# Gathering run 39's sums before its own scatter, and statistics one by one around output tiles, in a cross-attention and mixture-of-experts kernel

## The chip, the cores and the metric

The kernel runs on one core of a Trainium2 chip. The time is that of one execution on the device, in microseconds (us); of several executions the median counts. A profile is the record of one execution; its span goes from the first to the last instruction of the program. The engines are named as in the profile: PE is TensorE, PEld its weight loads, DVE is VectorE, ACT is ScalarE, POOL is GpSimd, SP is SyncE, which here only issues DMAs. The DMA queue q1 holds what SyncE issues, q0 what GpSimd issues; both are served by the same 16 DMA engines.

## The reference

The input x has 32 sequences of 128 tokens with 256 features, 4096 tokens in all. Layer 1 is a cross-attention on the normalised x, with 16 heads, added to x. Layer 2 normalises again, and sends each token through its best two of eight experts:

```
x = x + xattn(layernorm(x), ctx)                       # 16 heads of 64, then Wo, bo
r = layernorm(x)
logits = r @ Wg + bg
top2_vals, top2_idx = top_k(logits, 2)
combine = softmax(top2_vals) on the two experts
h = gelu(r @ W1[e] + b1[e])                            # 256 -> 1024, for each expert e
y = h @ W2[e] + b2[e]                                  # 1024 -> 256
out = sum over e of combine[e] * y[e]
result = x + layer_norm(r + out, gamma, beta)
```

All is in float32. So the last step of every token needs the outputs of both of its experts: the sum r + out, its mean and variance over 256 features, and then gamma, beta and the residual x.

## The kernel before, in words

The tokens are worked on in eight blocks of 512 for the attention and the choice of experts. Then each token is placed twice in a table in DRAM (`slots`), by expert. The feed-forward part takes that table in *runs*: a run is 256 tokens (two tiles of 128) or 128 tokens (one tile) of one expert. There are 46 runs, numbered in the order in which they are worked on. The last three (43 to 45) are spare and are skipped by a branch unless they are needed, so the last one that counts is number 42 (`L` in the code, `MAIN` is 43). `X` is 37. Runs 37 to 42 have two tiles each.

A run goes through four functions. `fetch_rows` has GpSimd gather the run's tokens by index. `turn` transposes them on TensorE and copies them out on VectorE (`xT`, L439). `hidden` multiplies by W1 and puts gelu on ScalarE (`hT`, L451 and L454). `outputs` multiplies by W2 (L470); VectorE adds the bias (L481), scales by the token's weight (L487), and GpSimd issues an indirect DMA which adds the tile's rows to a table of sums in DRAM, `total` (L490). This is called the scatter below. The scatters of two runs may not overlap, since a token may be in both: each run's scatter waits for the landing of the run before it. The two tiles of one run hold different tokens. `outputs` can be given a function (`then`) which is called once, behind its first tile.

The order on every engine is the order of the code: each engine works through a list written out by hand. PSUM has eight banks, which the tiles of all products use in turn.

The end of the kernel, where the change lies, runs two things side by side. On one hand, the blocks are finished: `load_sums` loads a block's 512 rows from `total` (L1105, SyncE), `measure` takes their statistics on VectorE (four pairs of L148 and L149, and a power of -0.5 on GpSimd, L155), `scale` normalises on ScalarE (L1128), and `put_out` multiplies by gamma and adds the residual on VectorE (L1134, L1141) and stores. For blocks 3 and 4 the residual is already in the output, so `put_out` stores with an accumulating DMA from GpSimd (L1145); for the others it is a plain store from SyncE (L1142).

On the other hand, blocks are loaded before all runs are added. Blocks 0 to 2 hold tokens of which runs up to 36 have all outputs; they are loaded behind run 36's scatter. Blocks 3 to 7 are loaded behind run 38's scatter. The tokens of the four runs 39 to 42 are then corrected one by one after the block's rows are written: for each of these runs `fetch_own` gathers the sums of its tokens from `total` (two indirect DMAs on GpSimd, L1166), `rate` takes their statistics (with a power on GpSimd, L1187), `patch` finishes them on VectorE (L1196, L1198), and `send` writes them over the output rows (two indirect DMAs on GpSimd, L1209, which wait for the writes of the run before). The residual rows are gathered earlier into `bases`. Runs 41 and 42 already spare a detour: run 41's outputs are kept in `kept_rows` and added on VectorE to sums gathered before its scatter (L1320), and run 42 is never scattered at all but added on VectorE (L484).

The order in the code around the change is: run 37's `hidden`, block 0's and 1's `measure`, run 37's `outputs` with block 2's `measure` inside; run 38's `hidden` and `outputs`; loads of blocks 3 to 7; run 39's `hidden` and `outputs` with measures of blocks 3 to 5; run 40's `hidden`, measures of blocks 6 and 7; the gather of run 39's sums; run 40's `outputs`; `rate` and `patch` of run 39; the gather of run 40's sums, `send` of run 39, the gather of run 41's sums; run 41's `hidden` and `outputs`; and so on to `send` of run 42.

Of the kernel before, what the change touches and what calls it, by code (L numbers as in the profile page):

```python
# [12 lines left out]
ALU = mybir.AluOpType  # L13
# [12 lines left out]
def kernel(  # L26
# [19 lines left out]
    nc = tc.nc  # L46
# [67 lines left out]
    total = dram.tile([NTOK + P, D], F32, name="total")  # L114
# [30 lines left out]
    def tile_stats(pool, src, mv, t):  # L145

        st = pool.tile([P, 6], F32, name="bnst", tag="bnst")
        nc.vector.bn_stats(st, src[:, t, :])  # L148
        nc.vector.bn_aggr(mv[:, t, :], st)  # L149

    def deviation(pool, mv, rstd):

        ve = pool.tile([P, TB], F32, name="ve", tag="ve")
        nc.vector.tensor_scalar_add(ve, mv[:, :, 1], LN_EPS)  # L154
        nc.gpsimd.tensor_tensor(rstd, ve, mhalf, ALU.pow)  # L155
# [18 lines left out]
    def bank(name):  # L174
        return ps.tile([P, TB, P], F32, name=name, tag="bank")

    def flat(t):
        return t.rearrange("p t s -> p (t s)")
# [5 lines left out]
    MAIN = NRUN - SPARE  # L184
# [223 lines left out]
    def reach(rows, m):  # L408

        return rows[: OLD * TOK, :] if m < AHEAD else rows  # L410
# [19 lines left out]
    def turn(m):  # L430

        nt, xg = order[m][2], rows_of.pop(m)
        px = flat(bank("px"))
        for k in range(KD):
            for t in range(nt):
                j = k * nt + t
                nc.tensor.transpose(px[:, ts(j, P)], xg[:, t, ts(k, P)], ident)  # L437
        xT = a2.tile([P, KD, nt * P], F32, name=f"xT{m}", tag="kT")
        nc.vector.tensor_copy(xT.rearrange("p k s -> p (k s)"), px[:, : KD * nt * P])  # L439
        turned[m] = xT  # L440
# [18 lines left out]
    added = []  # L459

    def outputs(m, then=None):


        nt, who, hT = order[m][2], whos.pop(m), hiddens.pop(m)
        mine = []
        w1t, bt, w2t = weights.pop(m)
        for t in range(nt):
            py = flat(bank("py"))
            for c in range(NHC):
                nc.tensor.matmul(  # L470
                    py[:, :D],
                    lhsT=hT[c // (NHC // 2)][:, c % (NHC // 2), ts(t, P)],
                    rhs=w2t[:, c, :],
                    start=(c == 0),
                    stop=(c == NHC - 1),
                )
            if m == MAIN - 2:
                y = kept_rows[:, t, :]
            else:
                y = f3.tile([P, D], F32, name=f"y{m}_{t}", tag="y")  # L480
            nc.vector.tensor_tensor(y, py[:, :D], bt[:, NHC:], ALU.add)  # L481
            if m == MAIN - 1:
                z = own(sums, m)[:, t, :]
                nc.vector.scalar_tensor_tensor(z, y, who[:, t, 1:2].bitcast(F32), z, ALU.mult, ALU.add)  # L484
                then(t)
                continue
            nc.vector.tensor_scalar(y, y, who[:, t, 1:2].bitcast(F32), None, ALU.mult)  # L487
            if t > 0:
                nc.gpsimd.memset(apart, 0.0)
            add = nc.gpsimd.indirect_dma_start(  # L490
                out=reach(total, m),
                out_offset=bass.IndirectOffsetOnAxis(ap=who[:, t, 0:1], axis=0),
                in_=y,
                in_offset=None,
                compute_op=ALU.add,
            )


            for other in mine:
                tc.declare_no_dep(add.ins, other.ins, reason="tokens of their own")  # L500
            for other in added:
                tc.add_manual_dep(add.ins, other.ins.name, DATA, reason="the run before")
            mine.append(add)
            if t == 0 and then is not None:
                then()
        added[:] = mine
# [540 lines left out]
    hidden(1)  # L1047
    turn(2)
    outputs(0, lambda: turn_gate(last))
    gate(last)  # L1050
    fetch_weights(3)
# [11 lines left out]
    route(last)  # L1063
    next(rest)
    outputs(1, lambda: next(rest))
    fetch_weights(4)
    next(rest)
# [32 lines left out]
    def load_sums(blk):  # L1100

        tag = ("qT", "xnT", "rows", "wkm", "wvm")[blk // 2 if blk < 6 else blk - 3]
        acc = (a2 if blk < 6 else aw).tile([P, TB, D], F32, name=f"acc{blk}", tag=tag)
        accs[blk] = acc
        got = nc.sync.dma_start(out=acc, in_=block(total, blk))  # L1105
        for other in added:
            tc.add_manual_dep(got.ins, other.ins.name, DATA, reason="these sums are complete")
        return got

    def measure(blk):  # L1110

        scales[blk] = (
            fs.tile([P, TB, 2], F32, name="mv3", tag="mv3"),
            fs.tile([P, TB], F32, name="rstd3", tag="rstd3"),
        )
        mv, rstd = scales[blk]
        for t in range(TB):
            tile_stats(fs, accs[blk], mv, t)
        deviation(fs, mv, rstd)
# [30 lines left out]
    L = MAIN - 1  # L1150
    X = MAIN - (NREST - EARLY + AHEAD)
    assert L - PATCH >= X + 1
    out_rows = out.rearrange("b s d -> (b s) d")
    sums = aw.tile([P, PATCH, 2, D], F32, name="sums", tag="wo_sb")
# [4 lines left out]
    def own(t, m):  # L1159
        return t[:, m - (L - PATCH + 1)]  # L1160

    def fetch_own(t, table, m, complete=()):

        who = last_who.setdefault(m, whos.get(m))
        for i in range(2):
            got = nc.gpsimd.indirect_dma_start(  # L1166
                out=own(t, m)[:, i, :],
                out_offset=None,
                in_=table,
                in_offset=bass.IndirectOffsetOnAxis(ap=who[:, i, 0:1], axis=0),  # L1170
            )
            for other in complete:
                tc.add_manual_dep(got.ins, other.ins.name, DATA, reason="these sums are complete")
# [3 lines left out]
    def rate(m, tiles=slice(0, 2)):  # L1177

        z = own(sums, m)[:, tiles, :]
        n = z.shape[1]  # L1180
        mv = fs.tile([P, 2, 2], F32, name="mvp", tag="mvp")
        ve = fs.tile([P, 2], F32, name="vep", tag="vep")
        rstd = fs.tile([P, 2], F32, name="rstdp", tag="rstdp")
        for t in range(n):
            tile_stats(fs, z, mv, t)
        nc.vector.tensor_scalar_add(ve[:, :n], mv[:, :n, 1], LN_EPS)
        nc.gpsimd.tensor_tensor(rstd[:, :n], ve[:, :n], mhalf[:, :n], ALU.pow)  # L1187
        parts[m, tiles.start] = mv, rstd

    def patch(m, tiles=slice(0, 2)):  # L1190

        z, base = own(sums, m)[:, tiles, :], own(bases, m)[:, tiles, :]
        mv, rstd = parts.pop((m, tiles.start))
        n = z.shape[1]
        for t in range(n):
            nc.vector.scalar_tensor_tensor(z[:, t, :], z[:, t, :], mv[:, t, 0:1], gamma_sb, ALU.subtract, ALU.mult)  # L1196
        for t in range(n):
            nc.vector.scalar_tensor_tensor(  # L1198
                z[:, t, :], z[:, t, :], rstd[:, t : t + 1], base[:, t, :], ALU.mult, ALU.add
            )  # L1200

    def send(m):

        z = own(sums, m)
        mine = []
        for t in range(2):
            if t > 0:
                nc.gpsimd.memset(apart, 0.0)
            put = nc.gpsimd.indirect_dma_start(  # L1209
                out=out_rows,  # L1210
                out_offset=bass.IndirectOffsetOnAxis(ap=last_who[m][:, t, 0:1], axis=0),
                in_=z[:, t, :],
                in_offset=None,
            )
            for other in mine:
                tc.declare_no_dep(put.ins, other.ins, reason="tokens of their own")
            for other in sent + [stored[blk] for blk in range(OLD, NBLK)]:
                tc.add_manual_dep(put.ins, other.ins.name, DATA, reason="over what came before")
            mine.append(put)
        sent[:] = mine  # L1220
# [51 lines left out]
    run(X)  # L1272
    fetch_own(bases, resid, L)
    measure(0)
    measure(1)
    outputs(X, lambda: measure(2))
    assert X + 1 == L - 4
    fetch_weights(L - 2)
    run(L - 4)
# [4 lines left out]
    put_out(2)  # L1284


    for blk in range(OLD, NBLK):
        got = load_sums(blk)
    fetch_weights(L - 1, behind=got)
# [11 lines left out]
    measure(7)  # L1301
    scale(6)
    turn(L - 1)
    fetch_own(sums, total, L - 3, added)
    put_out(3)
    scale(7)
    outputs(L - 2, lambda: put_out(4))
# [2 lines left out]
    put_out(6)  # L1310
    patch(L - 3)
    put_out(7)
    fetch_own(sums, total, L - 2, added)
    send(L - 3)
    fetch_own(sums, total, L - 1, added)
    hidden(L - 1)
    turn(L)
    outputs(L - 1)
    rate(L - 2)
    nc.vector.tensor_tensor(own(sums, L - 1), own(sums, L - 1), kept_rows, ALU.add)  # L1320
    rate(L - 1)
    patch(L - 2)
    send(L - 2)
    fetch_own(sums, total, L, added)
    patch(L - 1)
    hidden(L)

# [52 lines left out]
```

## Time and profile before

| | us |
|---|---|
| median of 3 runs | 1143.42 |
| lowest and highest | 1140.73, 1146.16 |
| the profiled execution | 1143.15 |
| its span | 1141.30 |
| PE busy | 1105.3 (97%) |
| DVE busy | 598.1 (52%) |
| ACT busy | 461.1 (40%) |
| POOL busy | 313.4 (27%) |

The 1.85 us between the profiled execution and its span lie around the program. The busy shares are means over a long attention part, a long feed-forward part and a short end. Times within the profile are given from the start of the span. In a line of a timeline the first number is the start, the second the length, and what stands in brackets at the end is how long the engine had been idle and what ended that. A DMA that GpSimd issues shows two things: the time in which GpSimd works on the issue, and the landing, when its data is there; the second comes later.

### The profile page before, as it was taken

The numbers are of one execution on the slowest core, as the hardware profiler recorded it, in microseconds if no ns is written. First come the engines' busy times: TensorE is split into PE (matmuls) and PEld (weight loads), VectorE is DVE, ScalarE is ACT, GpSimd is POOL, SyncE is SP. The second block draws the span as 40 slices with busy tenths as digits, with TensorE's granted clock in tenths as the row PEclk, the third lists the DMA queues.
The fourth block names the chain that finished last, engine by engine and source line by source line (L and its number), as shares of the span: only waits on it lengthen the run. The fifth ranks groups of instructions, "written<-read, shape, count | busy, mean of one in ns | idle before, by whom it ended". The sixth has DMA issues, their size and how long they took to land.

```text
span 1141.3 us, 19129 instructions
## 1 busy us (share of the span) xinstructions
PE 1105.3 (97%) x6805; PEld 855.3 (75%) x6805; DVE 598.1 (52%) x1512; ACT 461.1 (40%) x1608; POOL 313.4 (27%) x379
## 2 busy tenths in 40 slices
PE   7999999999999999999999999999999999999982
PEld 3666757667666676676678889999889889987872
DVE  3876776776867777768666451122211111113753
ACT  2565454543554544536443223333233233224530
POOL 1000003021030030210404355343333343454455
PEclk9999999999999999999999999999999999999987
DMA  9400001110110001001133849899998878889882
GB/s 305 147 13 19 35 4 20 38 16 6 38 20 21 18 2 37 2 1 39 18 118 98 259 96 330 259 333 329 285 267 245 250 218 240 270 255 291 258 201 54
DMA packets 129632, 155.67 MB, mean 136 GB/s; under 512 B 21952, under 2 KB 114304, under 8 KB 129536
## 3 DMA queue, kind: packets, MB, share of 16 engines
q1 hardware_dynamic: 111520, 131.54, 35.3%
q0 software_dynamic: 17024, 21.84, 9.5%
q8 instruction: 55, 0.90, 0.4%
q10 hardware_dynamic: 992, 1.05, 0.3%
q14 instruction: 41, 0.34, 0.1%
HBM read 125.07 MB, written 29.33 MB: 135 GB/s over the span
## 4 chain that ended last, share of the span: by engine, by line
PE 86%; DMA 7%; POOL 2%; DVE 2%; issue 2%; ACT 1%; POOLq 0%; SPq 0%; DVEq 0%; ACTq 0%
PE py L470 16%; PE ph L451 15%; PE pw L789 10%; PE pq L695 10%; PE pss L716 5%; PE pk L660 5%; PE po L775 5%; PE ptp L754 5%; PE pv L684 5%; DMA total<-y,who 4%; PE pv L671 3%; PE pk L654 3%; PE ptx L617 1%; PE px L437 1%; DMA acc<-total 1%
## 5 line engine op out<-in xcount | busy, mean ns | idle before, releaser
L454 ACT ACTIVATE hT<-ph,b 128x256 f32<-128x256 f32 (+1 forms) x344 | 146.1, 429 | 334.2 <-PE ph L451 320.3
L730 ACT ACTIVATE pr<-pss,nmax 128x128 f32<-128x128 f32 x512 | 179.1, 401 | 211.4 <-DVE nmax L726 211.4
L451 PE MATMUL ph<-xT,w 128*128 128x256 f32 (+1 forms) x1376 | 247.0, 338 | 7.4 <-DVE xT L439 4.8
L451 PEld LDWEIGHTS ph<-xT,w 128*128 128x128 f32 x1376 | 220.3, 192 | 30.8 <-DVE xT L439 5.2
L470 PE MATMUL py<-w,hT 128*128 128x256 f32 x1088 | 242.2, 379 | 0.0
L470 PEld LDWEIGHTS py<-w,hT 128*128 128x128 f32 x1088 | 203.4, 190 | 25.9
L490 POOL DMA_INDIRECT total<-y,who x64 | 106.2, 1659 | 212.4 <-DVE y L487 134.1
L730 ACT ACTIVATION_READ_ACCUMULATOR pr<-pss,nmax 128x1 f32 x512 | 123.9, 242 | 0.0
L695 PE MATMUL pq<-xnT,wq_sb 128*128 128x512 f32 x256 | 115.2, 592 | 0.3 <-DVE xnT L618 0.3
L789 PE MATMUL pw<-wo_sb,oT 128*128 128x256 f32 x512 | 113.3, 379 | 0.0
L481 DVE TENSOR_TENSOR y<-py,b 128x256 f32<-128x256 f32 x66 | 27.9, 423 | 155.0 <-PE py L470 155.0
L439 DVE COPY xT<-px 128x512 f32<-128x512 f32 (+1 forms) x43 | 24.8, 578 | 156.2 <-PE px L437 156.2
L789 PEld LDWEIGHTS pw<-wo_sb,oT 128*128 128x128 f32 x512 | 96.0, 190 | 12.6 <-issue 0.2
L155 POOL TENSOR_TENSOR rstd<-ve,mhalf 128x4 f32<-128x4 f32 x24 | 24.9, 1038 | 261.0 <-DVE ve L154 258.2
L695 PEld LDWEIGHTS pq<-xnT,wq_sb 128*128 128x128 f32 x256 | 48.6, 190 | 61.3 <-issue 59.0
L129 POOL DMA_INDIRECT slots<-info,ati x64 | 62.7, 980 | 113.5 <-DVE ati L924 95.4
L744 DVE TENSOR_TENSOR pr<-pr,rden 128x512 f32<-128x512 f32 x128 | 88.5, 692 | 4.4
L726 DVE TENSOR_REDUCE nmax<-pss 128x4 f32<-128x512 f32 x128 | 79.5, 683 | 18.5 <-PE pss L716 18.5
L422 POOL DMA_INDIRECT xg<-xrows,who x64 | 63.3, 989 | 28.7 <-issue 12.9
L754 PEld LDWEIGHTS ptp<-ident,pr 128*128 128x128 f32 x512 | 57.9, 141 | 17.0 <-issue 16.1
L663 DVE COPY kT<-pk 128x512 f32<-128x512 f32 x64 | 44.2, 691 | 44.1 <-PE pk L660 42.9
L716 PE MATMUL pss<-kT,qT 64*128 64x128 f32 x1024 | 65.8, 278 | 0.0
(178 smaller groups left out, 1201.9 us busy)
## 6 DMA issues: line engine op xcount, KB each, us to landing
w<-in_L_ffn_W_dram SPq DMA_DIRECT2D x86, 1024.0 KB, 8.4
b<-biases SPq DMA_DIRECT2D x43, 132.0 KB, 5.1
xres<-in_x_dram SPq DMA_DIRECT2D x8, 512.0 KB, 7.8
xrows<-rows SPq DMA_DIRECT2D x8, 512.0 KB, 2.8
total<-rows SPq DMA_DIRECT2D x8, 512.0 KB, 4.1
resid<-xres SPq DMA_DIRECT2D x8, 512.0 KB, 10.7
acc<-total SPq DMA_DIRECT2D x8, 512.0 KB, 5.8
ctx<-in_ctx_dram SPq DMA_DIRECT2D x8, 384.0 KB, 6.4
```

The costliest lines, as they stand in the source:

```text
L422: nc.gpsimd.indirect_dma_start(out=xg[:, t, :], out_offset=None, in_=reach(xrows, m), in_offset=bass.IndirectOffsetOnAxis(ap=whos[m][:, t, ...
L451: nc.tensor.matmul(ph[:, : nt * P], lhsT=w1t[:, k, ts(c, P)], rhs=xT[:, k, :], start=(k == 0), stop=(k == KD - 1))
L454: nc.scalar.activation(hT[c // half][:, c % half, :], ph[:, : nt * P], AF.Gelu, bias=bt[:, c : c + 1])
L470: nc.tensor.matmul(py[:, :D], lhsT=hT[c // (NHC // 2)][:, c % (NHC // 2), ts(t, P)], rhs=w2t[:, c, :], start=(c == 0), stop=(c == NHC - 1),)
L490: add = nc.gpsimd.indirect_dma_start(out=reach(total, m), out_offset=bass.IndirectOffsetOnAxis(ap=who[:, t, 0:1], axis=0), in_=y, in_offse ...
L695: nc.tensor.matmul(pq, lhsT=wq_sb[:, k, ts(2 * q + c, P)], rhs=xnTs[blk][:, k, :], start=(k == 0), stop=(k == KD - 1),)
L716: nc.tensor.matmul(pss[2 * c + h][:, t, :], lhsT=qT[ts(h, DH), c, ts(t, S)], rhs=kT[ts(h, DH), c, ts(t, S)], start=True, stop=True,)
L726: nc.vector.tensor_reduce(nmax, pss[h], AX.X, ALU.max, negate=True)
L730: nc.scalar.activation(pr[:, t, :], pss[h][:, t, :], AF.Exp, bias=nmax[:, t : t + 1], accum_out=den[:, t : t + 1],)
L744: nc.vector.tensor_tensor(pr, pr, rden.unsqueeze(2).to_broadcast([P, TB, S]), ALU.mult)
L754: nc.tensor.transpose(pt[:, t, :], pr[:, t, :], ident)
L789: nc.tensor.matmul(pw[:, :D], lhsT=oTs[blk][:, k, ts(t, S)], rhs=wo_sb[:, k, :], start=(k == 0), stop=(k == NHP - 1),)
```

## The change

Three things change.

In the middle of run 37, block 1's statistics move from ahead of run 37's outputs to between its two tiles, and block 2's from between the tiles to behind them.

The gather of run 39's sums moves from behind the measures of blocks 6 and 7 to ahead of the loads of blocks 3 to 7, which is behind run 38's scatter and ahead of run 39's own. The gathered sums then lack run 39's outputs, so `outputs` adds each of its two tiles on VectorE to them. The scatter of run 39 itself stays, since later runs and their sums need it.

The order of GpSimd's last gathers and writes changes: the gathers of run 40's and run 41's sums follow each other; run 39's writes come behind run 41's outputs; the gather of run 42's sums comes ahead of run 40's writes instead of behind them.

```
@@ outputs
             nc.vector.tensor_scalar(y, y, who[:, t, 1:2].bitcast(F32), None, ALU.mult)
+            if m == MAIN - 4:
+                z = own(sums, m)[:, t, :]
+                nc.vector.tensor_tensor(z, z, y, ALU.add)
             if t > 0:
                 nc.gpsimd.memset(apart, 0.0)
@@
     measure(0)
-    measure(1)
-    outputs(X, lambda: measure(2))
+    outputs(X, lambda: measure(1))
+    measure(2)
@@
     put_out(2)
+    fetch_own(sums, total, L - 3, added)
     for blk in range(OLD, NBLK):
         got = load_sums(blk)
@@
     turn(L - 1)
-    fetch_own(sums, total, L - 3, added)
     put_out(3)
@@
     put_out(7)
-    fetch_own(sums, total, L - 2, added)
-    send(L - 3)
-    fetch_own(sums, total, L - 1, added)
+    for m in range(L - 2, L):
+        fetch_own(sums, total, m, added)
     hidden(L - 1)
     turn(L)
     outputs(L - 1)
+    send(L - 3)
     rate(L - 2)
     nc.vector.tensor_tensor(own(sums, L - 1), own(sums, L - 1), kept_rows, ALU.add)
     rate(L - 1)
     patch(L - 2)
+    fetch_own(sums, total, L, added)
     send(L - 2)
-    fetch_own(sums, total, L, added)
     patch(L - 1)
     hidden(L)
```

More of the change, by code (lines that the diff above doesn't have):

```diff
@@ L487, in outputs @@
             nc.vector.tensor_scalar(y, y, who[:, t, 1:2].bitcast(F32), None, ALU.mult)
+            if m == MAIN - 4:
+                z = own(sums, m)[:, t, :]
+                nc.vector.tensor_tensor(z, z, y, ALU.add)
             if t > 0:
@@ L1274 @@
     measure(0)
-    measure(1)
-    outputs(X, lambda: measure(2))
+    outputs(X, lambda: measure(1))
+    measure(2)
     assert X + 1 == L - 4
@@ L1284 @@
     put_out(2)
+    fetch_own(sums, total, L - 3, added)
     for blk in range(OLD, NBLK):
@@ L1303 @@
     turn(L - 1)
-    fetch_own(sums, total, L - 3, added)
     put_out(3)
@@ L1312 @@
     put_out(7)
-    fetch_own(sums, total, L - 2, added)
-    send(L - 3)
-    fetch_own(sums, total, L - 1, added)
+    for m in range(L - 2, L):
+        fetch_own(sums, total, m, added)
     hidden(L - 1)
@@ L1318 @@
     outputs(L - 1)
+    send(L - 3)
     rate(L - 2)
@@ L1322 @@
     patch(L - 2)
+    fetch_own(sums, total, L, added)
     send(L - 2)
-    fetch_own(sums, total, L, added)
     patch(L - 1)
```

## The prediction

> **What bounds the kernel now.** I began with the page's busy rows.
>
> ```profile
> PE 1105.3 (97%) x6805; PEld 855.3 (75%) x6805; DVE 598.1 (52%) x1512; ACT 461.1 (40%) x1608; POOL 313.4 (27%) x379
> ```
>
> TensorE carries the kernel as a whole, but only until about 1040 us. The order of the instructions is the same before and after as far as run 37, so everything is decided in the last 100 us, and there I read the chain of waits, then TensorE's and GpSimd's timelines.
>
> ```profile
> 1078.66 8.07 DMA total<-y,who
> ...
> 1087.52 0.29 POOL sums L1166
> 1087.81 1.56 issue
> 1089.37 4.02 DMA sums<-total,who
> ...
> 1094.24 2.69 POOL total L490
> 1096.93 1.40 POOL out_dram L1145
> ...
> 1098.64 6.04 DMA total<-y,who
> ```
>
> This is the chain of waits (start, length, what). Run 39's second scatter lands at 1086.73, the gather of run 39's sums follows and lands at 1093.39, and only then may run 40's scatter start, because it writes the table that the gather reads. Run 40's second scatter lands at 1104.67. From there to the end at 1141.30 the chain stays on GpSimd and its DMAs.
>
> ```profile
> 1045.90 1.13 PE L451 MATMUL ph<-xT,w 128*128 128x256 f32 x4 [0.63 <-DVE y L481]
> 1048.95 1.13 PE L451 MATMUL ph<-xT,w 128*128 128x256 f32 x4 [1.93 <-DVE y L481]
> 1105.02 9.36 PE L451 MATMUL ph<-xT,w 128*128 128x256 f32 x32 [4.84 <-DVE xT L439]
> ```
>
> TensorE's timeline: its three late stalls. The first two are banks that run 37's outputs hold while VectorE is busy with the statistics of blocks 0 to 2.
>
> ```profile
> q0 software_dynamic: 1515, 1.63, 57.2%
> q1 hardware_dynamic: 2382, 2.74, 38.6%
> ```
>
> DMA queues from 1085 to 1105 us (packets, MB, share of 16 engines): together 95.8%. GpSimd waits there, but the DMA engines don't.
>
> **The change, part by part.** The sum is made against the profiled execution: 1143.15 us, of which 1141.30 are the span; the median of the runs, 1143.42, is 0.27 above it.
>
> *Statistics around run 37's tiles.* Nothing is added. Block 0's statistics end at 1043.07, so the first output tile (0.42 + 0.35) is done at 1043.9 instead of 1046.2; with block 1's statistics (2.3, from 1043.07 to 1045.4) the second follows at about 46.95 instead of 1049.28. TensorE's stall of 0.63 goes, that of 1.93 shrinks to about 0.2: TensorE is 2.4 earlier. On the path lies run 37's scatter. Its first half also needs the three block loads, of which the third lands 7.7 after 1036.29, at 1044.00; a landing reaches GpSimd's next issue 0.8 later (1086.73 to 1087.52), so it goes at 1044.85. The second half, behind one power operation (1.04), goes at 1047.8 instead of 1049.93: 2.1 earlier. Block 2's power operation comes later by the same exchange, at about 1050.5; its reader stands ahead of run 38's first tile, which TensorE finishes at 1051.5, so about 1 us covers it. Will the landing follow? The engines are 95% busy from 1040 to 1060, and run 40's weights move earlier too. The scatter issued at 1046.67 landed within 0.6 of a 1 MB load issued 6.4 before it, so scatters are served between the weights, not after them. I take 2.1; the other end is 0. Run 38's scatter, gated by that landing, then lands at 1062.9 instead of 1065.05.
>
> *The gather of run 39's sums, moved ahead.* GpSimd issues its two halves (0.98 each) behind run 38's scatter, waiting for it until 1063.75 and done at 1066. Queued behind them are the power operations of blocks 3 and 4, before at 1071.63: 3 us of cover. On the DMA engines 0.25 MB go in among the 2.5 MB of five block loads, which run at about 0.38 MB per us: 0.7 later for the last load. So run 39's first scatter, which waits for that load, goes 1.4 earlier, at 1074.3. The nearest rows for the gather's landing are the two gathers of residual rows issued beside block loads at 1035.93 and 1037.18: 6.5 each. That gives 1070.3 and 1071.6; VectorE wants the first at about 1073. Cover: 1.4 to 2.7.
>
> *The two additions.* 128x256 each, 0.42 by the row of L481. The scatter doesn't read them, but the second tile, the next blocks' statistics and the transposed rows of run 41 stand behind them on VectorE: 0.42 and 0.84, against about 1.8 that VectorE gains there. Run 39's second half then goes at 1077.2, and with 8.07 lands at 1085.3. GpSimd operations beside two-input work of VectorE are long in this trace: the scatter at 1094.24 took 2.69 against a median of 1.62. I charge nothing, since GpSimd waits for loads when the additions run. The Trainium skill ("SBUF — State Buffer", Who interferes with whom) speaks against the change here: a VectorE instruction with two SBUF inputs fully blocks a GpSimd instruction that reads SBUF. By that rule the sum below would be up to 0.8 smaller; the 2.69 agrees with it, and nothing in this trace shows it for an addition of this size.
>
> *The wait removed.* From run 39's landing to run 40's first scatter 7.51 pass now; without the gather it is the 0.85 of a hand-off: 6.66 on GpSimd, and with the 1.4 above 8.1. But the DMA engines must follow. From 1093 to 1096 the accumulating store of a block runs alone: 441 packets in 3 us, so 3.5 for its 512, and 0.87 for a scatter of 128. Two stores and two scatters are 8.7 us of all 16 engines. The hardware queue has 4.8 more (76.9% of 1086.7 to 1093: the rest of run 42's weights and block 5's store). Now the gather's wait keeps the first store (issued at 1090.34) behind the weights; after, it is issued at about 1083.6, into them. 1085.3 + 8.7 + 4.8 is 1098.8, and about 0.5 to the landing: 1099.3 for run 40's second scatter instead of 1104.67, so 5.4 of the 8.1. If stores and scatters were not held up by weights, it would be 8.1; if all went in the order of issue with block 6's store (1.4) and the idle gaps kept, about 3.
>
> *The tail.* From that landing (0) in rows of before: four gathers 1.3 apart from 0.8 on, the last landing 2.7 after its issue, at 7.4; run 41's scatter 2.0 later (1114.96 to 1116.99) and 1.9 on; now run 39's two writes until 15.6, the two power operations until 17.6, run 42's gather 17.8 and 19.1 (before 20.2), run 40's writes 20.4 and 21.7, landing at 24.3. Run 41's write must follow that landing: 25.1, against 25.55 before. The 2.8 that the gather gains are mostly turned into this new wait. With the second write 1.3 behind the first instead of 1.57 the gain is 0.7 (ends: 0.3, and 1.6 if run 41's scatter follows in 0.8).
>
> TensorE: without the late scatter the transposed rows of run 42 are copied at about 1097 instead of 1104.3, so the stall of 4.84 and the slow 9.36 go. Run 42's first output tile is then ready 10 us before its gathered sums: no further gain.
>
> Sum: 5.4 + 0.7 = 6.1, and 1143.15 - 6.1 = 1137.0.
>
> **The rivals.**
>
> *GpSimd's order alone counts* (stores and scatters are not held up by weights): 8.1 + 0.7 = 8.8, 1134.3. For it: run 37's scatter between the weights. Against: 95.8% busy. Chance 0.17.
>
> *The DMA engines take nearly all back* (order of issue): 3 + 0.3, 1139.8. For it: the hardware queue's landings of 9 to 13 us for weights in this stretch, and 8.07 for the scatter among them. Against: scatters overtook weights. Chance 0.13.
>
> *Slower: the gather starves.* Place: the first addition, in VectorE's order ahead of run 39's second tile, waits for a gather that competes with five block loads and then run 41's weights. Each us beyond 1073 moves run 39's second scatter and all behind it by one. The gain of 6.1 is gone at a landing of 1079, 15 us after the first half's issue; the kernel is slower by over 0.5% from 1085, 21 us after it, and at 1149 there. The longest landing near it is 12.9 (a weight load), the longest of a GpSimd gather beside loads 6.5. Chance 0.09.
>
> That the change doesn't do what it says can be excluded for the order: the gather stands ahead of run 39's scatter on GpSimd's list, the additions behind run 39's tiles on VectorE's.
>
> **How the numbers follow.** The forecast, DMA engines deciding, has 0.61, between 1134.5 and 1139.5. A measurement of this kernel tells about 0.5% from no change, 5.7 us, so faster means below 1137.7; the forecast is only just there. Of its 0.61 I put 0.39 below and 0.22 above; with the first rival that makes 0.56 faster; with the second 0.35 same; 0.09 slower. The range from 1132 to 1142 holds the forecast and both milder rivals with their ends (below, 8.1 and the tail's 1.6; above, 3 and the tail's 0.3, less up to 2 where run 37's scatter lands no earlier).
>
> **What would show it.** Right: no gather between 1080 and 1095; TensorE's stalls at 1045 and 1047 under 0.3 together and none at run 42's hidden layer; run 40's first scatter within 1 us of run 39's landing; an accumulating store issued near 1084 that lands later than its 6.8 now; run 40's second scatter landing 4 to 7 earlier; run 41's writes waiting for run 40's. Wrong: VectorE waiting for gathered sums in the first addition, or the two accumulating stores landing as fast as before.

## The result

The changed kernel takes 1134.22 us (median of 5 runs, 1133.13 to 1135.27) against 1143.42 before: a ratio of 0.992 with a 95% interval from 0.9898 to 0.9941. It is faster, as forecast, and 2.8 us below the 1137.0 of the forecast. In two later comparisons, with more runs on each side, the ratio was 0.9944 (0.9933 to 0.9956) and 0.9942 (0.9928 to 0.9957), which is 6.5 and 6.7 us. So a part of the first 9.2 us is variation between executions, and the forecast of 6.1 us less is nearer to the repeated measurements than to the first one. How much of that nearness is luck is worked out below.

The page's busy rows of the changed kernel:

```profile
PE 1101.3 (97%) x6805; PEld 854.8 (75%) x6805; DVE 598.7 (53%) x1514; ACT 461.2 (41%) x1608; POOL 311.2 (27%) x379
```

The two additions are the two instructions that VectorE has more (1514 against 1512). The chain of waits (start, length, what):

```profile
1075.05 8.61 DMA total<-y,who
...
1083.78 0.70 issue
1084.49 1.76 POOL total L493
1086.24 1.41 POOL out_dram L1148
...
1087.96 10.28 DMA total<-y,who
...
1099.03 1.06 POOL sums L1169
...
1102.93 2.78 DMA sums<-total,who
...
1108.52 1.61 POOL total L493
1110.13 0.31 issue
1110.44 0.99 POOL out_dram L1212
```

Run 39's second scatter lands at 1083.66, and run 40's first is issued 0.83 later; 7.51 passed there before. Nothing gathers between 1080 and 1095. But run 40's second scatter now takes 10.28 to land, where it took 6.04. It lands at 1098.24, and from there the chain stays on GpSimd and its DMAs to the end at 1132.5, but for two stretches of VectorE's work (from 1105.81 and from 1117.20). TensorE's timeline where the three late stalls were:

```profile
1039.02 7.07 PE L451 MATMUL ph<-xT,w 128*128 128x256 f32 x32
...
1046.36 7.07 PE L470 MATMUL py<-w,hT 128*128 128x256 f32 x32
...
1096.03 7.07 PE L451 MATMUL ph<-xT,w 128*128 128x256 f32 x32
```

No line has an idle time in brackets: both stalls in run 38's hidden layer are gone, and run 42's takes 7.07 instead of 9.36 behind a wait of 4.84. On GpSimd's and VectorE's timelines the moved gather and the first addition:

```profile
1060.13 1.02 POOL L1169 DMA_INDIRECT sums<-total,who  x1 [3.18 <-DMA total<-y,who]
1061.45 0.98 POOL L1169 DMA_INDIRECT sums<-total,who  x1 [0.30 <-issue]
```

```profile
1070.37 0.42 DVE L490 TENSOR_TENSOR sums<-sums,y 128x256 f32<-128x256 f32 x1
```

In the trace the gather's halves land at 1066.49 and 1067.83, 6.4 after issue. The addition starts 3.9 after the first landing and waits for nothing.

For what follows the span is cut in two at B, the landing of run 40's second scatter, and counted from S, the issue of the first block load. S lies ahead of the first instruction that the change moves, and it already came 1.07 earlier in the profiled execution of the changed kernel (1034.25 against 1035.32). That 1.07 belongs to the execution, not to the change. Before, S to B is 69.35 and B to the end 36.63; after, 63.99 and 34.26. So the span's 8.80 are 1.07 ahead of S, 5.36 from S to B, and 2.37 from B to the end. The change is worth 7.7 between these two traces. A stretch of one trace is not exact to 1 us: two later kernels have the order of the kernel before up to B, and there S to B is 68.46 and 71.25 (the latter in an execution 4.4 above its kernel's median); two more traces of the changed kernel have 64.80 and 64.50.

### The profile page after: what moved, and what is told of

The parts are those of the page before. It is cut to its first block, busy times and chain, and to the rows that moved or that the text cites. A ratio compares the mean times of both kernels' runs of the same rounds, so it can differ in the third digit from the quotient of the medians.

```text
span 1132.5 us, 19133 instructions
## 1 busy us (share of the span) xinstructions
PE 1101.3 (97%) x6805; PEld 854.8 (75%) x6805; DVE 598.7 (53%) x1514; ACT 461.2 (41%) x1608; POOL 311.2 (27%) x379
## 5 line engine op out<-in xcount | busy, mean ns | idle before, releaser
L451 PE MATMUL ph<-xT,w 128*128 128x256 f32 (+1 forms) x1376 | 244.2, 336 | 0.0
L698 PEld LDWEIGHTS pq<-xnT,wq_sb 128*128 128x128 f32 x256 | 48.6, 190 | 61.3 <-issue 58.9
L757 PEld LDWEIGHTS ptp<-ident,pr 128*128 128x128 f32 x512 | 57.9, 141 | 17.0 <-issue 16.1
```

Source lines behind the costliest of these rows:

```text
L451: nc.tensor.matmul(ph[:, : nt * P], lhsT=w1t[:, k, ts(c, P)], rhs=xT[:, k, :], start=(k == 0), stop=(k == KD - 1))
L698: nc.tensor.matmul(pq, lhsT=wq_sb[:, k, ts(2 * q + c, P)], rhs=xnTs[blk][:, k, :], start=(k == 0), stop=(k == KD - 1),)
```

## The experiments

They ran in three sets of four, each set on a chip of its own with runs of the kernel before beside it: 1157.84 us (median) for the first set, 1140.74 for the second, 1156.10 for the third. Times are compared within a set; across sets only ratios and stretches of the span are. Where a trace lacks the record of a landing, B is put 0.8 ahead of the gather that waited for it, the hand-off of the chain above.

**Each part alone.** First the statistics around run 37's tiles.

```
-    measure(1)
-    outputs(X, lambda: measure(2))
+    outputs(X, lambda: measure(1))
+    measure(2)
```

> Only the statistics of blocks 1 and 2 move around run 37's tiles; gather and tail as before. Theory (the chain from run 37's scatter on moves as a whole): run 37's second scatter goes 2 to 3 us earlier, run 38's landing 2 to 4, and since every later step waits for the one ahead of it the end comes 2 to 3 us earlier, 1140.5 to 1141.5. Rival (the DMA engines, 95% busy, take it back): run 38's landing moves, the last block load and all behind it do not, 1143.

Measured: 1156.84 us, ratio 0.9988 (0.9977 to 0.9999), 1.0 us below the kernel before. S to B is 68.35, 1.0 less than in the trace of the kernel before, but only 0.1 less than in the tail's experiment below, which has the old order up to B and ran on the same chip. So the traces of this set leave open whether the gain reaches B. Then the gather with its two additions, nothing else:

```
+            if m == MAIN - 4:
+                z = own(sums, m)[:, t, :]
+                nc.vector.tensor_tensor(z, z, y, ALU.add)
...
+    fetch_own(sums, total, L - 3, added)
     for blk in range(OLD, NBLK):
...
     turn(L - 1)
-    fetch_own(sums, total, L - 3, added)
```

> Only the gather of run 39's sums moves ahead of its scatter, with the two additions; statistics and tail as before. Theory (DMA engines decide in the end): on GpSimd the wait of 6.7 between run 39's landing and run 40's scatter goes, 0.7 is paid for the gather among the block loads, and about 3 is given back because the accumulating stores of blocks 3 and 4 and run 40's scatter queue behind run 42's weights; run 40's second scatter takes 8 us or more to land instead of 6.0; end 2.5 to 4 us earlier, about 1140. Rival (GpSimd's order alone counts): 6 us earlier, 1137.4. Rival (the gather starves): VectorE waits in the first addition, 1145 or more.

Measured: 1154.69 us, ratio 0.9969 (0.9957 to 0.9982). S to B is 66.57, 2.8 less than before. Run 40's first scatter was issued 53.2 after S (1103.53 less 1050.35) against 58.9, so GpSimd gained 5.7, of which half was lost again up to the landing. Against the tail's experiment on the same chip the two gains are 4.1 and 1.9: smaller, and again about half is lost. Then the order of the last gathers and writes alone:

```
+    for m in range(L - 2, L):
+        fetch_own(sums, total, m, added)
...
     outputs(L - 1)
+    send(L - 3)
...
+    fetch_own(sums, total, L, added)
     send(L - 2)
-    fetch_own(sums, total, L, added)
```

> Only the order of GpSimd's last gathers and writes changes. As predicted: gain 0.7, because run 41's writes must wait for run 40's, 1142.7. From the trace of after: 2.4 from run 40's second landing to the end, if run 41's scatter follows its gather by 0.9 instead of 2.0, 1141.0. In both the landing of run 40's second scatter stays where it was.

Measured: 1154.42 us, ratio 0.9971 (0.9959 to 0.9983). B to the end is 34.24, the same as in the changed kernel, so the tail's part stands by itself: 2.4 against the trace of the kernel before, 2.2 against the two experiments above, which keep the old tail (36.4 each). The product of the three ratios is 0.9928, where the whole change has 0.992 to 0.9944: the parts add up within their intervals, and none needs another.

**Where the accumulating stores of blocks 3 and 4 stand.** In the changed kernel they are issued at 1081.23 and 1085.65, on GpSimd's queue ahead of run 40's first and second scatter. Here they are issued behind run 40's second scatter, by a function `add_out` that holds the line taken out of `put_out`:

```
 def put_out(blk):
...
-            stored[blk] = nc.gpsimd.dma_start(out=of_block(out, blk), in_=acc, accum_op=ALU.add)
...
     rate(L - 3)
+    for blk in ADDED:
+        add_out(blk)
     put_out(6)
```

> The changed kernel, with the accumulating stores of blocks 3 and 4 issued behind run 40's scatter and run 39's power operation instead of ahead of and between its halves. Theory (run 40's scatter is late because it stands behind these stores in GpSimd's DMA queue): run 40's second scatter is issued about 1 us earlier and lands after 7 to 8 us instead of 10.3, so 3 to 4 us earlier, and the gathers behind it queue a little behind the stores; end 2 to 4 us earlier than the changed kernel, about 1131. Rival (the load is what run 42's weights make of it): run 40's second scatter still takes about 10 us, end within 1 us of the changed kernel, 1134.

Measured: 1147.18 us, ratio 0.9911 (0.9898 to 0.9924). GpSimd's timeline:

```profile
1102.97 1.57 POOL L493 DMA_INDIRECT total<-y,who  x1 [0.26 <-DVE bnst L148]
1105.42 2.74 POOL L1150 DMA_DIRECT2D out_dram<-acc  x2
1108.46 1.36 POOL L1171 DMA_INDIRECT sums<-total,who  x1 [0.30 <-issue]
...
1112.70 0.95 POOL L1171 DMA_INDIRECT sums<-total,who  x1 [0.30 <-issue]
1119.52 1.63 POOL L493 DMA_INDIRECT total<-kept_rows,who  x1 [5.88 <-DVE sums L1327]
```

The gather at 1108.46 must follow the landing of run 40's second scatter, and it no longer waits: the scatter landed in at most 4.7, instead of 10.28. A part of the stores' time is only moved: the gathers now stand behind them, the last one takes 6.02 to land by the chain of waits instead of 2.78, and run 41's scatter waits 5.88. S to B is 57.2 and B to the end 37.9, together 95.1, where three traces of the changed kernel have 98.3 to 99.1. No changed kernel ran in this set; the ratio lies below its 0.9944 and 0.9942 on two other chips, but its interval overlaps that of the first measurement (0.992).

The second set has the changed kernel itself, and two more places for the stores:

> The changed kernel itself, for comparison on this chip. Its three parts alone gave 0.9988, 0.9969 and 0.9971 on one chip. If they add up (each shortens another link of one chain) it is 0.9928; the first measurement of it was 0.992 (0.9898 to 0.9941). If the parts hid one another, it would be nearer to 0.995.

Measured: 1134.23 us, ratio 0.9944 (0.9933 to 0.9956); S to B 64.80, B to the end 34.27. In the next kernel the residual of blocks 3 and 4 is added on VectorE, and they are stored plainly by SyncE, as the other blocks are:

```
-    ADDED = (OLD, OLD + 1)
+    ADDED = ()
```

> The changed kernel with blocks 3 and 4 finished like the others: the residual is added on VectorE (two more operations of 1.22 us) and the block stored plainly by SyncE, so GpSimd's queue holds no accumulating store. Theory (run 40's scatter is late because these stores stand ahead of it in GpSimd's DMA queue): run 40's second scatter lands 6 to 7 us earlier than in the changed kernel, as it did with the stores behind it, and now nothing stands ahead of the gathers; about 2.4 are given back if VectorE is late for the transposed rows of run 42. End 4 to 7 us earlier than the changed kernel, ratio to before 0.986 to 0.988. Rival (two more VectorE operations cost what they save): as the changed kernel, 0.992.

Measured: 1129.46 us, ratio 0.9898 (0.9884 to 0.9912): 4.8 us below the changed kernel on the same chip, and the lowest ratio of all versions. S to B is 59.90. GpSimd's timeline at the scatter and the gather that waits for it:

```profile
1088.52 1.57 POOL L493 DMA_INDIRECT total<-y,who  x1 [0.26 <-issue]
...
1095.98 1.20 POOL L1169 DMA_INDIRECT sums<-total,who  x1 [3.12 <-DMA total<-y,who]
```

The scatter lands in 6.7. The same stores on the hardware queue still take time of the 16 DMA engines, but less of it (see the last section), and no scatter stands behind them in GpSimd's queue. The edit changes both at once, the kind of store and its queue, so this run doesn't tell which of them counts. It also leaves out two stores well ahead of S, which put the residual into the output; the gain lies behind S all the same (94.4 from S to the end instead of 99.1). Last, the accumulating stores behind the four gathers:

```
     for m in range(L - 2, L):
         fetch_own(sums, total, m, added)
+    for blk in ADDED:
+        add_out(blk)
```

> The changed kernel with the two accumulating stores behind the gathers of run 40's and 41's sums on GpSimd. In the run with the stores behind run 40's scatter the gathers had to wait 5.9 us in the queue behind the stores. Theory (each DMA of GpSimd's queue is served behind those issued ahead): the gathers land 2.8 after their issue again, run 41's scatter is issued 4 us earlier than in that run, but is itself served behind what is left of the stores; end 2 to 6 us earlier than the changed kernel, ratio to before 0.987 to 0.990. Rival (queue order among GpSimd's DMAs does not matter): as in the run with the stores behind the scatter, 0.991.

Measured: 1132.32 us, ratio 0.9931 (0.9918 to 0.9944), which overlaps the changed kernel's. GpSimd's timeline:

```profile
1086.14 1.56 POOL L493 DMA_INDIRECT total<-y,who  x1 [0.27 <-DVE bnst L148]
1087.27 1.34 POOL L1192 TENSOR_TENSOR rstdp<-vep,mhalf 128x2 f32<-128x2 f32 x1
1091.03 1.90 POOL L1171 DMA_INDIRECT sums<-total,who  x1 [2.42 <-DMA total<-y,who]
...
1096.73 2.82 POOL L1150 DMA_DIRECT2D out_dram<-acc  x2
...
1101.81 1.55 POOL L493 DMA_INDIRECT total<-kept_rows,who  x1 [0.26 <-DVE sums L1201]
1108.36 1.00 POOL L1214 DMA_INDIRECT out_dram<-sums,who  x1 [5.00 <-issue]
```

Without a store ahead of it run 40's second scatter lands in 4.1, and S to B is 57.19, 7.6 less than in the changed kernel. B to the end is 40.2, 5.9 more: run 41's two scatters stand behind the stores and land in 7.2 and 5.9 (3.8 and 3.9 in the changed kernel), and run 39's writes are issued 5.00 after GpSimd is done with those. The last store landed at 1106.35 and the last scatter at 1107.69; the profile names no releaser for this wait, so which of them it was for stays open. In every place that was tried the stores hold up what GpSimd issues next.

**The same edit without the change.** The kernel before with `ADDED = ()`:

> The kernel before with blocks 3 and 4 added on VectorE and stored plainly, nothing of the change. Theory (the accumulating stores hold up run 40's second scatter in both orders, by less in the kernel before, where it took 6.0 us to land and not 10.3): 1 to 4 us below the kernel before, less than the 4.8 us that the same edit gave on the changed kernel. Rival (the stores' cost is the same in both orders): 4.5 to 5.5 us below.

Measured: 1154.20 us, ratio 0.9984 (0.9974 to 0.9994): 1.9 us below the kernel before on its chip.

```profile
1110.73 1.69 POOL L490 DMA_INDIRECT total<-y,who  x1 [0.26 <-DVE sums L1196]
...
1115.66 1.76 POOL L1166 DMA_INDIRECT sums<-total,who  x1 [2.47 <-DMA total<-y,who]
```

This is GpSimd's timeline. The scatter lands in about 4.1 (1115.66 less 0.8 and less 1110.73) where it took 6.04 in the kernel before, and 6.67 to 7.01 in three other traces with the stores in the old order. A part of that is lost again: run 39's writes now wait 1.80 for a block's store, and B to the end is 37.1 instead of 36.4 to 36.6. By the times the stores cost 1.9 us in the old order and 4.8 in the changed one. So about 2.9 us of what the moved gather frees on GpSimd go to these two stores; the two figures come from two chips.

**The tail, taken apart.** The kernel before, with run 39's writes behind run 41's outputs, so that the four gathers follow each other; the gather of run 42's sums stays where it was:

```
+    for m in range(L - 2, L):
+        fetch_own(sums, total, m, added)
...
     outputs(L - 1)
+    send(L - 3)
```

> The kernel before, with run 39's writes alone moved: from between the gathers of run 40's and 41's sums to behind run 41's scatter. Half of the change's last part. By the prediction's account this moves run 41's scatter 2.6 earlier and gives 2.6 back ahead of the power operations: only the early landing counts, 0 to 0.3, ratio 0.9998 to 1. By the traces (run 41's scatter followed its gather by 2.0 with the old order and by 0.9 with the new one) it gains 1.2, ratio 0.999.

Measured: 1140.21 us, ratio 0.9991 (0.9983 to 1.0), beside 1140.74 for the kernel before: on the time alone this can't be told from no change. GpSimd's timeline:

```profile
1111.74 0.95 POOL L1166 DMA_INDIRECT sums<-total,who  x1 [0.30 <-issue]
1115.36 1.62 POOL L490 DMA_INDIRECT total<-kept_rows,who  x1 [2.67 <-DVE sums L1320]
```

The last gather lands at 1114.47 by the trace, and run 41's scatter follows 0.89 later. Before, it followed in 2.03. B to the end is 35.67, 0.96 less than before: a part of the tail's 2.4. The rest, 1.4, needs the gather of run 42's sums ahead of run 40's writes.

**Two terms by themselves, in the third set.** The changed kernel again, as the yardstick:

> The changed kernel again, as the yardstick of the three runs beside it. Theory: 6 to 9 us below the kernel before, its two additions 0.42 us each and waiting for nothing, run 40's second scatter about 10 us from issue to landing. Rival (a part of the earlier gain was the chip's own variation): under 4 us below.

Measured: 1149.40 us, ratio 0.9942 (0.9928 to 0.9957); S to B about 64.5. Then without the two additions:

```
-            if m == MAIN - 4:
-                z = own(sums, m)[:, t, :]
-                nc.vector.tensor_tensor(z, z, y, ALU.add)
```

> The changed kernel without the two VectorE additions; run 39's sums then lack run 39's own outputs, nothing else changes in the order. Theory (the additions lie beside TensorE's products and hold up nobody): within 1 us of the changed kernel. Rival (the additions delay VectorE's chain, or GpSimd's work beside them): the time falls by at least the two additions' 0.84 us and by up to 2 us, and run 39's scatters are issued that much earlier.

Measured: 1148.59 us, ratio 0.9934 (0.9919 to 0.9948); the intervals overlap. Run 39's scatters are issued 38.4 and 41.3 after S, with the additions 38.5 and 41.4. Run 40's first scatter is issued 50.6 after S in both. Block 3's accumulating store is issued 46.6 after S without them and 47.6 with them; the three traces of the changed kernel range from 47.0 to 48.2, so a delay of 1 there isn't shown. It lies off the path. Last, the changed kernel with the statistics in the old order:

```
-    outputs(X, lambda: measure(1))
-    measure(2)
+    measure(1)
+    outputs(X, lambda: measure(2))
```

> The changed kernel with the statistics in the order of the kernel before: gather and additions as changed, last gathers and writes as changed. Theory (the statistics' part feeds through run 37's second scatter to the path's end): 0.5 to 2 us slower than the changed kernel, run 37's second scatter issued about 2 to 3 us later against the first block load. Rival (with the gather gone from behind run 39's scatter, run 37's place no longer counts): within 0.5 us of it.

Measured: 1150.49 us, ratio 0.9953 (0.9937 to 0.9969), 1.1 us above the yardstick. Run 37's second scatter is issued 13.7 after S instead of 11.6, 2.1 later, and S to B is 1.0 longer. By time alone the intervals overlap. The two times (1.0 in the first experiment, 1.1 here) and this pair of traces agree on about 1.0 at B; the pair of the first set had 0.1.

## Why the prediction was right, and where it was off

**The number: right, in part by luck.** The sum was 5.4 up to run 40's second scatter and 0.7 in the tail. The tail gave 2.2 to 2.4. The two repeated measurements, 6.5 and 6.7 us, then leave about 4.1 to 4.5 for the landing. So one term was about 1 too large and the other 1.6 too small, and that 6.1 came out so near is partly that these two cancel.

**The 5.4 up to run 40's second scatter: right, by its own mechanism.** The working gave 8.1 on GpSimd and 5.4 at the landing, because stores and scatters would meet run 42's weights on the DMA engines. Counted from S, run 40's first scatter came 8.7 earlier (50.24 against 58.92) and the second's landing 5.36. DMA queues of the changed kernel from 1084.5 to 1098.3 us (packets, MB, share of 16 engines):

```profile
q0 software_dynamic: 1344, 1.31, 59.5%
q1 hardware_dynamic: 2258, 2.25, 48.3%
```

The two shares add to 107.8%, where they were 95.8% before. Packet times overlap in this count (q0 alone has 113% from 1093 to 1096 in the kernel before), so it is no strict limit, but it shows no stretch left empty. The store that the prediction placed near 1083.6 was issued at 1081.23 and took 10.3 to land instead of 6.8. The rival that counted GpSimd's order alone (1134.3) is nearest to the first measurement only by its sum. Its step, scatters not held up, is refuted by the 10.28, and by the kernel with the stores behind the gathers, where the same scatter needs 4.1. The rival in which the DMA engines take nearly all back (3.3 in all) is refuted by the repeated 6.5 and 6.7 us. The 5.36 itself is one pair of traces; any of the three old stretches less any of the three changed ones gives 3.7 to 7.3, so the size of 5.4 is confirmed only roughly.

**The statistics.** The scatter of run 37 was issued 2.1 earlier against S, as worked out, and the landing followed. Between the two first traces it looks like 3.0 (1049.93 to 1045.87, less 1.07); the pair on one chip shows 2.1. Of it about 1.0 is left at B by the times and by that pair; the prediction had carried all of the 2.1 on to run 39's scatter. Both stalls of TensorE went, as forecast.

**The gather and the additions.** The landing of 6.5, taken from the residual gathers beside block loads, was 6.4; the cover was 3.9 instead of 1.4 to 2.7, because run 38's second scatter landed 3.95 after its issue and the gather started earlier. The rival in which the gather starves needed a landing 15 us after issue before the gain was gone, and is refuted. The additions were charged nothing, and the kernel without them shows that this holds on the path. The Trainium skill ("SBUF — State Buffer", Who interferes with whom) would have GpSimd instructions that read SBUF blocked during such additions; by that rule up to 0.8 was at stake. No run here shows a delay of the path by it: the power operation beside the second addition takes 1.46 with the additions and 1.60 without them, in the third set.

**The tail: right in its mechanism, mis-sized.** The sum had 0.7 here; measured were 2.37 between the first traces and 2.2 to 2.4 with the tail's part alone. The term that failed is "run 41's scatter 2.0 later", a hand-off copied from a row of the old order. In the chain of the changed kernel the last gather lands at 7.48 after B (7.4 was worked out), but run 41's first scatter goes at 8.36 instead of 9.4, and the second at 10.28 instead of 11.3. The second step that was too dear are the two power operations, charged 2.0; the trace has them in 1.40. So run 42's gather goes at 16.1 instead of 17.8. The new wait came where it was forecast: run 41's writes stand behind the landing of run 40's, at 23.4 instead of 25.1.

```profile
1112.74 1.40 POOL L1190 TENSOR_TENSOR rstdp<-vep,mhalf 128x2 f32<-128x2 f32 x2
1114.32 1.03 POOL L1169 DMA_INDIRECT sums<-total,who  x1 [0.18 <-DMA out_dram<-sums,who]
...
1121.64 1.04 POOL L1212 DMA_INDIRECT out_dram<-sums,who  x1 [1.61 <-DMA out_dram<-sums,who]
```

These lines are GpSimd's timeline of the changed kernel. The prediction gave the short hand-off only as the upper end, 1.6; with the short hand-off, and the power operations at their measured length, the sum is 0.7 + 1.0 + 0.6, and that is the 2.4 measured within 0.1. What makes the hand-off 2.03 is visible one step further in GpSimd's timelines. The first line is the kernel before, the second the changed kernel, the third the kernel before with plain stores:

```profile
1116.99 1.61 POOL L490 DMA_INDIRECT total<-kept_rows,who  x1 [3.79 <-DVE mvp L149]
...
1106.60 1.62 POOL L493 DMA_INDIRECT total<-kept_rows,who  x1 [2.72 <-DVE sums L1323]
...
1127.98 1.62 POOL L490 DMA_INDIRECT total<-kept_rows,who  x1 [2.62 <-DVE sums L1320]
```

In the first two VectorE's addition of `kept_rows` starts 0.1 after the landing. In the short cases the scatter goes as soon as that addition is done (within 0.1). In the kernel before it goes 1.24 after it, when VectorE has also finished the statistics of run 41, which the scatter doesn't read. The three traces with the 2.03 all end that wait so. The order of the gathers is not the whole reason: the third line has the old order of gathers and writes, without accumulating stores, and its scatter follows the addition by 0.06. Why the scatter waits for the statistics in the kernel before stays open.

## What to carry to other kernels

A wait taken away on the issuing engine is worth what the transfers behind it can follow: price the queue of bytes that is then let loose, not only the engine's order, and look for a large transfer that the old wait kept out of the way. When such a transfer turns up ahead of a small one on the path, change how it is made before changing where it stands; here two accumulating stores cost 4.8 us against plain stores on the other queue. The two other places in GpSimd's order that were tried moved a part of the delay: one saved 1.9 us, not clear of noise, the other, by ratios from different chips, 1 to 4. And a hand-off copied from a row holds only for the program in which that row stood: look at what ended the wait.

## What the runs showed of the hardware

An accumulating packet is dear: from the two queue rows above, q0's 1344 packets, nearly all accumulating, took 98 ns of an engine each (59.5% of 13.8 us on 16 engines), and q1's 2258 took 47 ns, both at about 1 KB. The queue alone doesn't make the difference. From 1121.6 to 1130 in the changed kernel, q0 holds four plain writes of run 41 and run 42 and nothing else:

```profile
q0 software_dynamic: 192, 0.52, 18.0%
```

That is 47 ns of an engine for each KB (18.0% of 8.4 us on 16 engines, for 0.52 MB), in larger packets. What GpSimd issues behind such a store also lands late: a gather took 6.02 instead of 2.78, and a scatter 10.28 instead of 4.1, in the kernels that differ only in where the stores stand.
